# Order of the first two steps, place of the next x load, and time of the first group's norms in a four-layer kernel

## The chip, the cores and the metric

One core of one Trainium2 chip. The metric is device time in microseconds (us), median of 3 runs; lower is better. The program runs once from inputs in HBM to the output in HBM.

## What is computed

The input x is (T=4, B=8, N=512, D=512) in float32. Four layers, each `x = x + f(gn(x))`, where `gn` normalises over groups of two channels of axis 1 (4 groups) and the 512 x 512 plane:

```python
# layer 0, for each t and b: x is a 512 x 512 plane, 8 heads of 64
q, k, v = (lif(bn(gn(x) @ W.T)) for W in (Wq, Wk, Wv))     # spikes, 0 or 1
scores = q @ k.T / sqrt(512)                                # per head
scores = scores + bias_table[rel]                            # by distance of row and column
out = lif(bn((lif(scores @ v) * gate_scale + gate_shift) @ Wp.T))
x = x + out
x = x + conv13x13(gn(x))                                    # layer 1, one kernel per channel
x = x + quantised_conv3x3(gn(x))                            # layer 2, 8 to 8 channels
x = x + conv3x3(gn(x))                                      # layer 3, 8 to 8 channels
```

`lif` is a recurrence over t: `v = v + (x - v) / 2; spike = v >= 1; v = v * (1 - spike)`.

## The kernel before

Layer 0 takes the first 1840 us, and the change lies there. It runs over 32 steps, `steps = [(b, t) ...]` with t inner, so step n is plane b = n // 4, t = n % 4. A group is two planes b, that is 8 steps n.

Each step's products x W are made by `unit` (L566): two units "kv" (half of the rows of k and v each) and one unit "q". A unit uses a seven-product scheme on 2 x 2 blocks: it multiplies blocks of x, and sums of blocks, by blocks of W and sums of those. The seven products, in the order a1, a2, g7, b6, b5, e4, b3, go to PSUM tiles a, b, g, e, f, where ACT copies a running sum from one tile to another in between (L620 `a` from the constants, L625/L633 `b` from `a`, L643 `e` from `b`, L655 `f` from `b`), and DVE evicts the tiles into spikes (`evict`, L598 to L612). The sums of x are made by `sum_x` (L913 to L917, on DVE: first x5 and x7, then x6 and x3), those of W once by `sum_weights` (L387 to L390).

What a step needs beforehand: its x. `load` (L919) asks SP for it in four quarters (`xq`, L503, 4 times 256 KB, in pieces of 128 floats). The group statistics are counted from `xq` and from the other plane's rows (`xs`, L486) by DVE (L512), and `settle` (L869) ends in two small matmuls over the partitions (`gps_x`, L165) with DVE work between them. Then ACT normalises `xq` (L888, four instructions at slot 13 of the step before), DVE transposes it (L895, slots 14 and 17), and `sum_x` follows.

After every even n >= 2 comes `attend` for the two steps before: eight heads, each of 12 matmuls per table (`own_part`, L706) with a bias table `table_own` of 576 KB fetched from HBM (L436). Three tables are held. The first three heads' tables are there before the attention begins; that of head h + 3 is asked for when head h's matmuls are done. Below, "head 7" is the last of the eight. `project_out` (L773 to L834) is spread over slots of the two steps after it; ACT's copies L803 free the `xr` rows, whose buffers (pool `x0`, four tiles) the `xs` rows also use.

Once, at the start: `w_raw` is loaded and scaled (L358: v and k on DVE, q on GpSimd, POOL in the profile); `c_kv` and `c_step` (constants split in three bf16 parts, `shift_kv` L361, GpSimd; used by the matmul L650); `split_bias` (L392) makes the table of bias parts in HBM through DVE and DMAs on ACT's queue; `prepare_out` (L450) scales Wp during step 1, four row blocks of it in turn, each passed from ACT to GpSimd and back twice; `bands1` (L1084) builds layer 1's bands.

What sets the order: a scheduler places the instructions of each engine by data, buffers and the order in which the program calls them; `tc.issue_after(op)` keeps what is traced inside it behind `op` on `op`'s engine. All engines, and SP's and ACT's DMA queues, then work strictly in that order: an instruction that waits holds all those behind it. In a step, `for slot, op in enumerate(all_units(n))` gives the slots at which other work is traced.

Of the kernel before, what the change touches and what calls it, by code (L numbers as in the profile page):

```python
# [123 lines left out]
def network(ctx: ExitStack, tc: tile.TileContext, i: dict, out: bass.AP):  # L124
# [20 lines left out]
    def group_steps(  # L145
        stats, n_groups, n, mask, weights, psum, name, n_each=D // 2, bufs=2, then=None, share=None
    ):

        mean, m2 = stats[:, :, :, 1], stats[:, :, :, 2]
        gs = [P, n_groups]
        buf = small.tile([P, n_groups, n], F32, tag="gbuf", name=f"gbuf_{name}", bufs=1)
        part_sum = small.tile(gs, F32, tag="gsum", name=f"gsum_{name}")
        m = small.tile(gs, F32, tag=f"gmean_{bufs}", name=f"gmean_{name}", bufs=bufs)
        r = small.tile(gs, F32, tag=f"grstd_{bufs}", name=f"grstd_{name}", bufs=bufs)
        masks = mask.unsqueeze(1).to_broadcast([P, n_groups, n]) if mask is not None else None

        def over_partitions(src):
            nc.vector.tensor_reduce(part_sum, src, AX.X, ALU.add)  # L160
# [4 lines left out]
            nc.tensor.matmul(ps, lhsT=weights, rhs=part_sum, start=True, stop=True)  # L165
            yield
            return ps

        if mask is None:
            nc.vector.tensor_copy(m, (yield from over_partitions(mean)))  # L170
        else:
            nc.vector.tensor_mul(buf, mean, masks)
            nc.vector.tensor_copy(m, (yield from over_partitions(buf)))
        if then is not None:
            then(m)
        nc.vector.tensor_sub(buf, mean, m.unsqueeze(2).to_broadcast([P, n_groups, n]))
        nc.vector.tensor_mul(buf, buf, buf)
# [82 lines left out]
def layer0(  # L260
# [100 lines left out]
    def shift_kv(banks):  # L361
        rest = state.tile([3 * SQ, 2, HN], F32, tag="h_o", name="c_rest")
        for n in "kv":
            nc.vector.tensor_sub(
                rest[:, at_w[n], :], banks[n][: 3 * SQ, 1], c_kv[: 3 * SQ, at_w[n], :]
            )
        for z in range(3):
            for q in [slice(0, 3 * SQ)] if z == 0 else [slice(r * SQ, (r + 1) * SQ) for r in range(z, 3)]:
                nc.gpsimd.tensor_copy(c_step[q], rest[q])
                if z < 2:  # L370
                    nc.gpsimd.tensor_sub(rest[q], rest[q], c_step[q])


    def w_quarter(i, o):
# [7 lines left out]
    def sum_weights(first, end, engine):  # L382
# [7 lines left out]
        engine.tensor_sub(b12, b21, t2)  # L390

    def split_bias():  # L392

# [56 lines left out]
    def prepare_out():  # L450
# [2 lines left out]
        scratch = state.tile([P, 3, D], F32, tag="h_o", name="scale_wp")  # L453
        scale = scratch[:, 0, :]
        nc.scalar.copy(scale.rearrange("p (g v) -> p g v", g=PH), phases(along_free(a_rows, 3)))
        for k in range(NC):
            yield
            wp = scratch[:, 1 + k % 2, :]
            nc.scalar.mul(
                wp.rearrange("p (g v) -> p g v", g=PH), phases(wp_rows[k]), gate_scale[:, k : k + 1]  # L460
            )
            nc.gpsimd.tensor_mul(wp, wp, scale)
            yield
            nc.scalar.copy(wpT[0][:, k, :], wp)
            nc.gpsimd.tensor_sub(wp, wp, wpT[0][:, k, :].bitcast(F32))
            nc.scalar.copy(wpT[1][:, k, :], wp)
# [99 lines left out]
    def unit(kind, cc, n, got):  # L566
# [56 lines left out]
        if ahead:  # L623
            b = new("b")
            seeds.append(nc.scalar.copy(b, a).ins)  # L625
            mul(a, 2)
            evict(a, 0, 0)
            yield
        g = new("g")
        mul(g, 7, True)  # L630
        if not ahead:
            b = new("b")
            seeds.append(nc.scalar.copy(b, a).ins)  # L633
        twice.append(work.tile([P, 2, HN], F32, tag="twice", name="twice"))
# [4 lines left out]
        yield  # L639
        mul(b, 6)  # L640
        yield
        e = new("e")
        seeds.append(nc.scalar.copy(e, b).ins)  # L643
        if not ahead:
            mul(a, 2)
            evict(a, 0, 0)
            yield
        mul(b, 5)
        if kind == "kv":
            nc.tensor.matmul(  # L650
                b, lhsT=share, rhs=c_step, start=False, stop=True, skip_group_check=True
            )
        yield
        f = new("f")
        seeds.append(nc.scalar.copy(f, b).ins)  # L655
        mul(e, 4)
        evict(f, 1, 1)
        evict(e, 1, 0)
        yield
        mul(b, 3)  # L660
        evict(b, 0, 1)
        yield

    def shift_q(n):

# [187 lines left out]
    def first_norm(key):  # L853
# [3 lines left out]
        for first in (0, 2):  # L857
            with behind:
                next(steps)
            op = scale_weights("v", scales["v"], nc.vector, (first, first + 1))  # L860
            next(steps)
            behind = tc.issue_after(op)
        with behind:
            try:
# [89 lines left out]
    scales = {n: along_free(a_rows, "qkvp".index(n)) for n in "vkq"}  # L954
    scale_q = state.tile([P, D], F32, tag="h_p", name="scale_q")
    nc.scalar.copy(scale_q, scales["q"])
    with tc.issue_after(normed):
        load(0)
        second = load_x(1, 0, "xs")
# [4 lines left out]
    constants = {}  # L964
    for n in "kv":
        constants[n] = along_free(c_rows, "qkvp".index(n)).rearrange("p (o e) -> p o e", o=2)
        nc.scalar.copy(c_kv[:, at_w[n], :], constants[n][:, 0])
    normalise(0)
    transpose(0, 0)
    transpose(0, 1)  # L970
    scale_weights("k", scales["k"], nc.vector)
    sum_x(0, 0)
    summed = sum_x(0, 1)
    sum_weights(0, 2, nc.vector)
    scale_weights("q", scale_q, nc.gpsimd)
    sum_weights(2, 3, nc.gpsimd)

    def all_units(n):
        if n == 0:
# [16 lines left out]
    for n in range(last + 3):  # L996
# [10 lines left out]
        if n <= last:  # L1007
# [1 line left out]
                spikes = new_spikes()  # L1009
            spikes["k"] = spiking.tile([P, NC, D], F8, tag="k", name="k")  # L1010
            g, j = divmod(n, PAIR * T)
            if n > 0:
                with tc.issue_after(fetched[-1]) if n % 2 == 0 else ExitStack():
                    load(n + 1)
            if j == 2 and g > 0:
                norm1(g - 1, ps_1)
            if g == 0 and 0 < n < T - 1:
                statistics(0, n + 1, 0, as_rows(xs[n + 1]))
                statistics(0, n + 1, 1, load_x(1, n + 1, "xs"))
            while due:  # L1020
                settle(due.pop())
            if n > 0:
                next_group(n - 1)
        if n == 1:
            preparing = prepare_out()
            banding = bands1(tc, i, band1d, w_sum, eye, ps_1, state)
        for slot, op in enumerate(all_units(n)):
# [9 lines left out]
                    statistics(0, 1, 1, load_x(1, 1, "xs"))  # L1037
            if n == 0 and slot == 0:
                with tc.issue_after(summed):
                    shift_kv(constants)  # L1040
            if n == 0 and slot == 7:
                with tc.issue_after(potentials[1]), tc.issue_after(seeds[0]):
                    parts = split_bias()
                    next_group(-1)
                with tc.issue_after(loads[-1]):
                    for h in range(H):
                        nc.sync.dma_start(tables_x[h], table_rows(h, 0, 1))
# [2 lines left out]
                    shift_q(n - 1)  # L1050
            if n == 1:
                with tc.issue_after(seeds[-1]):
                    if slot % 2 == 0:
                        next(preparing, None)
                    if slot in (11, 19):
                        next(banding, None)
            if slot == 13 and n <= last:
                add_halves(spikes, steps[n][1])
                with tc.issue_after(seeds[-1]):
# [24 lines left out]
def bands1(tc, i, band1d, w_sum, eye, psum, state):  # L1084
# [8 lines left out]
    def part(n_part, n):  # L1093
# [5 lines left out]
    w1 = part(K1, B * n_w).rearrange("k (c d) -> k c d", c=B)  # L1099
    c13 = part(K1, PH * n_p).rearrange("k (f j) -> k f j", f=PH)  # L1100
    rows = part(K1, B)
    nc.scalar.dma_start(
        c13, i["c13"].rearrange("k (f j) -> k f j", f=PH)[:, :, (W1_OUT - 1) * PH :][:, :, :n_p]
    )
    nc.vector.memset(w1, 0.0)
    taps = w1[:, :, PH - 1 : PH - 1 + K1]
    nc.scalar.dma_start(taps, i["w1"].rearrange("k (c d) -> k c d", c=B))
    nc.scalar.dma_start(
        eye.rearrange("p s m -> p (s m)"), i["c128"][:K1_P, i["c128"].shape[1] - SHIFTS * M1 :]
    )  # L1110
    nc.vector.memset(zeros, 0.0)
    rest = band1d.rearrange("p (r m) -> p r m", r=W1_OUT)
    nc.scalar.dma_start(rest, zeros.unsqueeze(1).to_broadcast([K1_P, W1_OUT, P]))
    yield

    ps = psum.tile([n_p, P], F32, tag="misc", name="ps_band")
    for f in range(PH):
# [7 lines left out]
    nc.scalar.dma_start(  # L1125
        bass.AP(band1d.tensor, band1d.offset, [[row, n_p], [PH * row + P, W1_OUT], [1, P]]),
        band.unsqueeze(1).to_broadcast([n_p, W1_OUT, P]),
    )
# [625 lines left out]
```

## Time and profile before

| what | us |
|---|---|
| median of 3 runs | 2715.78 |
| lowest, highest | 2710.00, 2716.22 |
| the profiled execution's own time | 2710.35 |
| its span on the core | 2708.6 |
| layer 0: first matmul of a unit | 29.70 |
| first attention begins on PE (L706) | 134.98 |
| last attention's end, about | 1835 |

PE is TensorE, DVE VectorE, ACT ScalarE, POOL GpSimd, SP SyncE. In a timeline line stand the start, the duration of the merged run, engine, source line, operation, out<-in, shape and count; in brackets, the engine's idle time just before it and what ended it. An fp32 matmul instruction of 512 columns has two records here, so one product of a unit is "x4", 1.88 us. ACTq and SPq are the queues in which ACT and SP issue DMAs. Where DMA is named as releaser, the data landed last.

### The profile page before, as it was taken

The page shows a single profiled execution, that of the slowest core. Times are in us where ns is not written, and L with a number is a line of the kernel's source. Part 1 is how long each engine was busy: PE and PEld are TensorE (multiplying, and loading weights), DVE is VectorE, ACT ScalarE, POOL GpSimd, SP SyncE. Part 2 cuts the span into 40 slices and gives each one's busy share as a digit, 9 for nine tenths or more (in the row PEclk, how much of TensorE's full clock was granted, in tenths as well). Part 3 has the DMA queues.
Part 4 walks back from the last instruction along what each step waited for, and adds up shares of the span by engine and source line. Part 5 has one row for each costly group of instructions (what it writes and reads, how often), then busy time and mean ns, then how long its engine had stood idle before and what let it go on. Part 6 is the DMA issues. An engine that isn't in the chain of part 4 may idle for free. (4 is left out here: it accounts for less than half of the span.)

```text
span 2708.6 us, 49604 instructions
## 1 busy us (share of the span) xinstructions
PE 2599.6 (96%) x18124; PEld 1506.2 (56%) x18124; DVE 1918.7 (71%) x4054; ACT 1238.3 (46%) x2093; POOL 756.0 (28%) x2040
## 2 busy tenths in 40 slices
PE   7899999999999999999999999998999999689999
PEld 3566566665666656666567666664333333344447
DVE  7877878778688787877877768756555556665550
ACT  1454454555445545445554554543111211466663
POOL 4322224123132222312312322223111111454540
PEclk9999999999999999999999999998999999899999
DMA  5553443544435444354442442446877778567755
GB/s 135 154 145 97 131 128 105 139 113 113 126 98 147 109 121 134 79 149 107 125 126 71 118 108 81 122 118 152 219 188 213 207 217 219 141 191 210 212 164 154
DMA packets 420664, 385.02 MB, mean 142 GB/s; under 512 B 22675, under 2 KB 339843, under 8 KB 420307
## 3 DMA queue, kind: packets, MB, share of 16 engines
q1 hardware_dynamic: 361696, 306.46, 43.8%
q0 software_dynamic: 16448, 51.27, 5.2%
q10 hardware_dynamic: 42275, 24.12, 3.2%
q8 instruction: 142, 2.33, 0.4%
q14 instruction: 103, 0.84, 0.1%
HBM read 278.09 MB, written 103.67 MB: 141 GB/s over the span
## 5 line engine op out<-in xcount | busy, mean ns | idle before, releaser
L1192 PE MATMUL ps_conv<-x,bt 112*64 112x512 f32 x2048 | 451.5, 595 | 6.4 <-DMA x<-x 6.4
L823 POOL COPY x1s<-x1s 128x1 f32<-128x1 f32 x1000 | 187.9, 241 | 649.8 <-DVE x1s L811 636.8
L1192 PEld LDWEIGHTS ps_conv<-x,bt 112*64 112x64 f32 x2048 | 149.2, 135 | 297.9 <-issue 293.8
L787 PE MATMUL ps_out<-wp,so 128*128 128x512 f32 x1024 | 303.9, 440 | 5.9 <-ACT ps_out L784 4.0
L554 PE MATMUL ps_kv_a<-w_raw,x_raw 128*128 128x512 f32 x512 | 252.8, 612 | 13.9 <-DVE w_raw L358 9.2
L1199 ACT ACTIVATE xo<-ps_conv,off 128x512 f32<-128x512 f32 x128 | 87.7, 687 | 378.3 <-PE ps_conv L1192 315.6
L787 PEld LDWEIGHTS ps_out<-wp,so 128*128 128x128 f32 x1024 | 193.9, 191 | 108.8 <-ACT ps_out L784 38.8
L554 PE MATMUL ps_kv_b<-w_sums,x_sum 128*128 128x512 f32 x512 | 246.6, 602 | 4.8 <-DVE x_sum L916 2.8
L1632 PE MATMUL ps_conv<-x,band_t 32*32 32x512 f32 x6144 | 230.2, 597 | 1.0 <-ACT o L1672 1.0
L638 POOL TENSOR_TENSOR h_kv<-h_kv,twice 128x512 f32<-128x512 f32 x96 | 123.6, 1307 | 380.4 <-ACT twice L635 379.8
L706 PE MATMUL ps_own<-table_own,v 128*128 128x256 bf16 x1536 | 193.3, 275 | 24.1 <-DMA table_own<-bias_parts 21.1
L706 PEld LDWEIGHTS <-v 128*128 128x128 fp8e4 x1536 | 148.2, 98 | 66.7 <-DMA table_own<-bias_parts 32.5
L1214 POOL DMA_DIRECT2D x<-xo x128 | 71.4, 564 | 345.6 <-ACT xo L1199 337.3
L742 ACT COPY ps_f<-ps_own 64x512 f32<-64x512 f32 x256 | 142.9, 558 | 49.7 <-PE ps_own L706 21.6
L1527 DVE SCALAR_TENSOR_TENSOR x<-ps_conv,inv,x 128x512 f32<-128x512 f32 x128 | 95.2, 750 | 98.8 <-PE ps_conv L1491 90.1
L554 PEld LDWEIGHTS ps_kv_a<-w_raw,x_raw 128*128 128x128 f32 x512 | 96.8, 195 | 111.1 <-issue 95.3
L1632 PEld LDWEIGHTS ps_conv<-x,band_t 32*32 32x32 f32 x6144 | 118.1, 103 | 70.2 <-issue 47.1
L554 PEld LDWEIGHTS ps_kv_b<-w_sums,x_sum 128*128 128x128 f32 x512 | 95.9, 191 | 103.2 <-issue 85.0
L803 ACT COPY x1s<-xr 128x256 f32<-128x256 f32 x250 | 151.8, 659 | 1.6 <-DMA x<-x1s 1.6
L1154 DVE SCALAR_TENSOR_TENSOR bt<-band,r,eye 112x64 f32<-112x64 f32 x128 | 31.6, 370 | 165.5 <-PE ps_conv L1192 164.0
L1491 PE MATMUL ps_conv<-xq,band 64*64 64x512 bf16 x1536 | 125.7, 400 | 21.5 <-DVE x L1527 15.4
L783 ACT CAST so<-q 128x512 fp32r<-128x512 fp8e4 x128 | 78.9, 618 | 142.9 <-PE ps_out L787 138.9
(257 smaller groups left out, 5060.4 us busy)
## 6 DMA issues: line engine op xcount, KB each, us to landing
table_own<-bias_parts SPq DMA_DIRECT2D x128, 576.0 KB
x<-x SPq DMA_DIRECT2D x64, 917.0 KB
xq<-in_x SPq DMA_DIRECT2D x128, 256.0 KB
xr<-in_x SPq DMA_DIRECT2D x128, 256.0 KB
x<-x1s POOLq DMA_DIRECT2D x125, 262.0 KB, 2.8
out<-o SPq DMA_DIRECT2D x120, 256.0 KB
xs<-in_x SPq DMA_DIRECT2D x112, 256.0 KB
x<-x SPq DMA_DIRECT2D x128, 224.0 KB
```

The source lines that it names most:

```text
L554: mm = nc.tensor.matmul(ps, lhsT=x[:, kk, cc * P : (cc + 1) * P], rhs=w[:, :2, kk, :], start=start and kk == 0, stop=kk == 1, skip_group_c ...
L638: nc.gpsimd.tensor_add(h, c if t == 0 else h, twice[0])
L706: nc.tensor.matmul(out, lhsT=src[:, c, h].rearrange("p t e -> p (t e)"), rhs=table[:, z, u : u + HN], start=start and c == 0 and z == 0, s ...
L742: nc.scalar.copy(final[j][a][two * DH : (two + 1) * DH, :], rows[a * DH : (a + 1) * DH, :])
L787: nc.tensor.matmul(ps, lhsT=tokens[:, k, :], rhs=wpT[z][:, k, :], start=False, stop=k == NC - 1 and z == 1, skip_group_check=True,)
L803: op = nc.scalar.copy(halves[z][1], by_phase[:, two, :])
L823: nc.gpsimd.tensor_copy(x1[:, f, u : u + n], x1[:, fm, um - n + 1 : um + 1][:, ::-1])
L1192: mm = nc.tensor.matmul(ps[q * M1 : (q + 1) * M1, :], lhsT=bt[:, z, :], rhs=xt[:, w0 : w0 + N_PS1, z : z + NV], start=z == 0, stop=z == SH ...
L1199: nc.scalar.activation(xo[:, a, :], ps, AF.Identity, bias=off[:, t : t + 1])
L1491: mm = nc.tensor.matmul(ps[half, :], lhsT=w["band2"][halves[b], kind, dx, :], rhs=xq[halves[b], j % 2, dx : dx + PH, :], start=dx == 0 and ...
L1527: nc.vector.scalar_tensor_tensor(inner, ps, w["inv"], x, op0=ALU.mult, op1=ALU.add, accum_out=sums[:, 0, :] if summed else None,).ins
L1632: mm = nc.tensor.matmul(ps[c * QP : (c + 1) * QP, :], lhsT=band[g * QP : (g + 1) * QP, int(last), dx, :], rhs=src[:, dx : dx + PH, :], sta ...
```

## The change

1. Opening: `scale_weights("k")` is put ahead of the sums of x on DVE, and these behind it alternate with `sum_weights(0, 2)`; the constants' matmuls (`along_free`) and copies for q and c are spread into the first norm; `shift_kv` stands behind those; the scaling and sums of q's weights are called behind `shift_kv`'s last GpSimd instruction.
2. `split_bias` and the `table_x` loads go from slot 7 to slot 14 of step 0; `next_group(-1)` stays at slot 7.
3. `prepare_out` takes two row blocks at a time, so that the GpSimd work of one lies beside ACT's work of the other; it ends before slot 14.
4. The DMAs of `bands1` go from ACT's queue to SP's.
5. At even n, `load(n + 1)` is called after `next_group(n - 1)` and stands on SP behind its first `xs` load, where there is one; before, it stood behind the last table fetched so far. At odd n it is still called first.
6. For n = 1 and 2 the norm of step n + 1 is no longer settled where its rows are asked for; for the first group's two planes (n < 8) all open norms are settled at slot 9. `yield` now hands out the matmul to which this is tied.
7. In `unit`, the copy L633 is called ahead of the g product.

In the built program this moves on SP, at the eleven attentions that have an `xs` load behind them (n = 2 to 22): before, five tables, the four `xq`, one `xs`, three tables among the other `xs`; after, eight tables, `xs`, `xq`, `xs`, `xq`, `xs`, `xs`, `xq`, `xq`. At the four attentions from n = 24 on nothing moves.

```diff
@@ group_steps
-            nc.tensor.matmul(ps, lhsT=weights, rhs=part_sum, start=True, stop=True)
-            yield
+            mm = nc.tensor.matmul(ps, lhsT=weights, rhs=part_sum, start=True, stop=True)
+            yield mm.ins
@@ prepare_out
-        for k in range(NC):
+        def scaled(k):
+            nc.scalar.mul(
+                wps[k].rearrange("p (g v) -> p g v", g=PH), phases(wp_rows[k]),
+                gate_scale[:, k : k + 1],
+            )
+            nc.gpsimd.tensor_mul(wps[k], wps[k], scale)
+
+        def first_part(k):
+            nc.scalar.copy(wpT[0][:, k, :], wps[k])
+            nc.gpsimd.tensor_sub(wps[k], wps[k], wpT[0][:, k, :].bitcast(F32))
+
+        def second_part(k):
+            nc.scalar.copy(wpT[1][:, k, :], wps[k])
+
+        for k in (0, 2):
             yield
...
+            scaled(k)
             yield
...
+            first_part(k)
+            scaled(k + 1)
+            yield
+            second_part(k)
+            first_part(k + 1)
+            yield
+            second_part(k + 1)
@@ first_norm
-            next(steps)
+            with tc.issue_after(next(steps)):
+                if first == 0:
+                    scales["q"] = along_free(a_rows, 2)
+                    nc.scalar.copy(scale_q, scales["q"])
+                else:
+                    for n in "kv":
+                        ps = along_free(c_rows, "qkvp".index(n))
+                        constants[n] = ps.rearrange("p (o e) -> p o e", o=2)
+                        nc.scalar.copy(c_kv[:, at_w[n], :], constants[n][:, 0])
@@ layer0, opening
-    scale_weights("k", scales["k"], nc.vector)
-    sum_x(0, 0)
-    summed = sum_x(0, 1)
-    sum_weights(0, 2, nc.vector)
-    scale_weights("q", scale_q, nc.gpsimd)
-    sum_weights(2, 3, nc.gpsimd)
+    op = scale_weights("k", scales["k"], nc.vector)
+    with tc.issue_after(op):
+        sum_x(0, 0)
+        sum_x(0, 1)
+    summed = sum_weights(0, 2, nc.vector)
@@ layer0, at the start of step n
-            if n > 0:
-                with tc.issue_after(fetched[-1]) if n % 2 == 0 else ExitStack():
-                    load(n + 1)
+            if n % 2 == 1:
+                load(n + 1)
...
-            if g == 0 and 0 < n < T - 1:
-                statistics(0, n + 1, 0, as_rows(xs[n + 1]))
-                statistics(0, n + 1, 1, load_x(1, n + 1, "xs"))
             while due:
                 settle(due.pop())
             if n > 0:
+                at = len(loads)
                 next_group(n - 1)
+                if n % 2 == 0:
+                    with tc.issue_after(loads[at] if at < len(loads) else fetched[-1]):
+                        load(n + 1)
+                if g == 0 and n < T - 1:
+                    statistics(0, n + 1, 0, as_rows(xs[n + 1]))
+                    statistics(0, n + 1, 1, load_x(1, n + 1, "xs"), later=True)
@@ layer0, slots
-                    shift_kv(constants)
+                    last_step = shift_kv(constants)
+                with tc.issue_after(last_step):
+                    scale_weights("q", scale_q, nc.gpsimd)
+                    sum_weights(2, 3, nc.gpsimd)
             if n == 0 and slot == 7:
                 with tc.issue_after(potentials[1]), tc.issue_after(seeds[0]):
+                    next_group(-1)
+            if n == 0 and slot == 14:
+                with tc.issue_after(potentials[-1]), tc.issue_after(seeds[-1]):
                     parts = split_bias()
-                    next_group(-1)
...
-                    if slot % 2 == 0:
+                    if slot < 14:
                         next(preparing, None)
-                    if slot in (11, 19):
+                    if slot in (12, 19):
                         next(banding, None)
+            if n <= last and slot == 9 and steps[n][0] < PAIR:
+                with tc.issue_after(op):
+                    while due:
+                        settle(due.pop(0))
@@ bands1, all five DMAs
-    nc.scalar.dma_start(
+    nc.sync.dma_start(
```

More of the change, by code (lines that the diff above doesn't have):

```diff
@@ L368, in shift_kv @@
             for q in [slice(0, 3 * SQ)] if z == 0 else [slice(r * SQ, (r + 1) * SQ) for r in range(z, 3)]:
-                nc.gpsimd.tensor_copy(c_step[q], rest[q])
+                op = nc.gpsimd.tensor_copy(c_step[q], rest[q])
                 if z < 2:
                     nc.gpsimd.tensor_sub(rest[q], rest[q], c_step[q])
+        return op.ins
     def w_quarter(i, o):
@@ L389, in sum_weights @@
         engine.tensor_sub(t2, b22, t1)
-        engine.tensor_sub(b12, b21, t2)
+        return engine.tensor_sub(b12, b21, t2).ins
     def split_bias():
@@ L455, in prepare_out @@
         nc.scalar.copy(scale.rearrange("p (g v) -> p g v", g=PH), phases(along_free(a_rows, 3)))
-        for k in range(NC):
-            yield
[L458 to L462, printed above, removed]
-            yield
-            nc.scalar.copy(wpT[0][:, k, :], wp)
-            nc.gpsimd.tensor_sub(wp, wp, wpT[0][:, k, :].bitcast(F32))
-            nc.scalar.copy(wpT[1][:, k, :], wp)
+        wps = [scratch[:, 1 + k % 2, :] for k in range(NC)]
+        def scaled(k):
[10 more added lines that the diff above has]
+        for k in (0, 2):
+            yield
+            scaled(k)
+            yield
+            first_part(k)
[5 more added lines that the diff above has]
+            second_part(k + 1)
         yield
@@ L625, in unit @@
             seeds.append(nc.scalar.copy(b, a).ins)
-            mul(a, 2)
+            op = mul(a, 2)
             evict(a, 0, 0)
-            yield
+            yield op
         g = new("g")
-        mul(g, 7, True)
         if not ahead:
@@ L633, in unit @@
             seeds.append(nc.scalar.copy(b, a).ins)
+        op = mul(g, 7, True)
         twice.append(work.tile([P, 2, HN], F32, tag="twice", name="twice"))
@@ L638, in unit @@
             nc.gpsimd.tensor_add(h, c if t == 0 else h, twice[0])
-        yield
-        mul(b, 6)
-        yield
+        yield op
+        yield mul(b, 6)
         e = new("e")
@@ L644, in unit @@
         if not ahead:
-            mul(a, 2)
+            op = mul(a, 2)
             evict(a, 0, 0)
-            yield
-        mul(b, 5)
+            yield op
+        op = mul(b, 5)
         if kind == "kv":
-            nc.tensor.matmul(
+            op = nc.tensor.matmul(
                 b, lhsT=share, rhs=c_step, start=False, stop=True, skip_group_check=True
-            )
-        yield
+            ).ins
+        yield op
         f = new("f")
         seeds.append(nc.scalar.copy(f, b).ins)
-        mul(e, 4)
+        op = mul(e, 4)
         evict(f, 1, 1)
         evict(e, 1, 0)
-        yield
-        mul(b, 3)
+        yield op
+        op = mul(b, 3)
         evict(b, 0, 1)
-        yield
+        yield op
     def shift_q(n):
@@ L953, in layer0 @@
     c_rows = as_rows_of(c_half.rearrange("p n c -> p (n c)"), rows[:, 1])
-    scales = {n: along_free(a_rows, "qkvp".index(n)) for n in "vkq"}
+    scales = {n: along_free(a_rows, "qkvp".index(n)) for n in "vk"}
+    constants = {}
     scale_q = state.tile([P, D], F32, tag="h_p", name="scale_q")
-    nc.scalar.copy(scale_q, scales["q"])
     with tc.issue_after(normed):
@@ L963, in layer0 @@
         statistics(0, 0, 1, second)
[L964 to L967, printed above, removed]
     normalise(0)
@@ L1106, in bands1 @@
     taps = w1[:, :, PH - 1 : PH - 1 + K1]
-    nc.scalar.dma_start(taps, i["w1"].rearrange("k (c d) -> k c d", c=B))
-    nc.scalar.dma_start(
+    nc.sync.dma_start(taps, i["w1"].rearrange("k (c d) -> k c d", c=B))
+    nc.sync.dma_start(
         eye.rearrange("p s m -> p (s m)"), i["c128"][:K1_P, i["c128"].shape[1] - SHIFTS * M1 :]
@@ L1112, in bands1 @@
     rest = band1d.rearrange("p (r m) -> p r m", r=W1_OUT)
-    nc.scalar.dma_start(rest, zeros.unsqueeze(1).to_broadcast([K1_P, W1_OUT, P]))
+    nc.sync.dma_start(rest, zeros.unsqueeze(1).to_broadcast([K1_P, W1_OUT, P]))
     yield
@@ L1124, in bands1 @@
     row = W1_OUT * P
-    nc.scalar.dma_start(
+    nc.sync.dma_start(
         bass.AP(band1d.tensor, band1d.offset, [[row, n_p], [PH * row + P, W1_OUT], [1, P]]),
```

## The prediction

> **What bounds the kernel.** I read the page first. PE is busy for 96% of the span, so only PE's idle time and slow matmuls can be won.
>
> ```profile
> PE 2599.6 (96%) x18124; PEld 1506.2 (56%) x18124; DVE 1918.7 (71%) x4054; ACT 1238.3 (46%) x2093; POOL 756.0 (28%) x2040
> ...
> PE   7899999999999999999999999998999999689999
> ...
> PEclk9999999999999999999999999998999999899999
> ```
>
> The thin slices are the first three and those behind layer 0. The change reaches only layer 0, so I cut that by stage: to the first attention, its first pair of steps, the attentions whose SP order moves, the rest.
>
> ```profile
> 0.00:135.00 135.00, 107.00 (x340) 60.98 (x341) 104.80 (x208) 37.18 (x60) 49.24 (x43) 0.97 0.59 145
> 135.00:262.00 127.00, 119.22 (x531) 77.80 (x530) 96.72 (x202) 61.26 (x107) 34.04 (x86) 0.96 0.42 113
> 262.00:1330.00 1068.00, 1050.33 (x4629) 689.76 (x4627) 855.61 (x1791) 553.67 (x964) 278.82 (x790) 1.00 0.45 122
> 1330.00:1830.00 500.00, 489.73 (x2180) 323.15 (x2179) 368.10 (x767) 262.46 (x458) 135.18 (x372) 1.00 0.40 107
> ```
>
> The second number is the length, the third PE's busy time: 28.0 us idle before the first attention, 7.8 behind it, 17.7 in the long stretch. PE's waits in 262 to 1330 name the last:
>
> ```profile
> PE ps_own L706 <- DMA table_own<-bias_parts: 12.5, 12, 2.9
> ```
>
> So the prize is two piles: about 28 us at the start, and bias tables that come late. PE's timeline of the start shows the first pile, with what held it (idle time in the bracket):
>
> ```profile
> 29.70 3.75 PE L554 MATMUL ps_kv_a<-w_raw,x_raw 128*128 128x512 f32 x4 [9.16 <-DVE w_raw L358]
> 41.88 1.99 PE L554 MATMUL ps_kv_a<-w_raw,x_raw 128*128 128x512 f32 x4 [1.05 <-ACT ps_kv_b L625]
> 79.67 3.56 PE L554 MATMUL ps_kv_a<-w_raw,x_raw 128*128 128x512 f32 x4 [2.40 <-ACT ps_kv_a L620]
> 106.14 0.38 PE L165 MATMUL gps_x<-gsum_x,avg 128*128 128x1 f32 x2 [2.15 <-DVE gsum_x L160]
> 124.47 2.00 PE L560 MATMUL ps_q_b<-x_sum,w_sums 128*128 128x256 f32 x8 [2.35 <-ACT ps_q_e L643]
> ```
>
> **Tables.** In the attention that begins at 702.0, head 7's table is asked for at 714.27, the four xq 0.5 us behind it:
>
> ```profile
> 714.27 0.36 SPq L436 DMA_DIRECT2D table_own<-bias_parts  x1
> ```
>
> and PE's timeline shows where it is waited for:
>
> ```profile
> 721.89 2.74 PE L706 MATMUL ps_own<-table_own,v 128*128 128x256 bf16 x12 [2.86 <-DMA table_own<-bias_parts]
> ```
>
> Here a rule speaks against the change. The Trainium skill (DMA: Bandwidth & Descriptors, section Queues, rings and completion order) says that on each DMA engine descriptors are consumed in ring order; then xq, issued later on SP's ring, could not delay the table, and moving it would give nothing. The row: DMA stands nearly still at 713.5 (15 to 23 GB/s, so all earlier tables have landed), and from 714.4 until PE goes on at 721.9 some 1.87 MB move, of which heads 6 and 7 are 2 x 576 KB. So about 0.7 MB of xq went ahead of the table's last bytes; at the 200 to 220 GB/s of that stretch this is 3.3 us, more than the wait of 2.86. I follow the row.
>
> With xq behind the tables, head 7's 576 KB flow alone: latency 1.5 us, then at the 340 to 370 GB/s seen at 714.6 some 1.7 us, landing near 718 where PE asks at 719.0. The new companion, the next pair's first table, is asked for only when head 5's matmuls are done (717.1), so its bytes begin near 718.6. Head 7's waits in the eleven attentions that change: 2.25, 1.76, 0.58, 0.21, 1.17, 2.86, 0.38, 0.67, 0, 2.26, 0 = 12.1 us. Waits of heads 5 and 6 (1.37, 0.58, 0.46 ...) stay, as do those from 1330 on (0.81, 0.36, 1.61, 0.78, 2.12): nothing is reordered there.
>
> What a wait costs beyond itself: after 2.25 and 2.86 us of idling, 12 matmuls took 2.74 instead of 1.48 us, twice 1.26. The Trainium skill (TensorE: Matmul & The Clock Gate, Part 1) would have the clock fall only after an idle window of about 3.4 us; by it the pile is 12.1, by the row 14.6. The row decides, though after 2.26 us at 1166.99 it was 1.52. With a tenth kept back: **-13 us**, from 0 to -15.
>
> What xq then costs. Its first quarter goes out behind xs 1, which waits for ACT's first L803; its last behind xs 4. Before, in the attention from 370 on, the last xs went out at 404.31 (the two there take 0.94), so the last xq goes at about 406 instead of 384 and lands by 409. Its reader is ACT:
>
> ```profile
> 418.16 2.94 ACT L888 ACTIVATE xq<-xq,shift,grstd_x 128x512 f32<-128x512 f32 x4
> ```
>
> Nine us of cover, so nothing is paid; without it, each us late is a us of PE in each of eleven steps. Behind xq on SP wait the xr loads and the small rows L831; xr stood at 408.29 anyway.
>
> **The opening.** Scaling k comes ahead of the four sums (25.49 to 28.15) and c_rest (0.74): the first product starts at 26.3 instead of 29.70, **-3.4**. Its slow clock (3.75 for x4 against 1.88) stays. The split of the bias leaves the kv units: ACT no longer stands behind the bias_table DMA (6.69 us, to 41.26), **-1.1**; the two xq quarters of step 1 which waited 15.3 us for the same DMA come early, and DVE has some 5 us less there, so the gps_x waits of 0.90 and 0.72 go, **-1.6**.
>
> Two new lateness risks. First, c_rest on DVE now stands behind the sums of W: GpSimd's c_step chain begins at 37.4 instead of 28.96. Before it took 11.0 us, of which 5.84 were two casts beside DVE's sums, where one such cast later took 0.75; without that, 6.4. It ends between 43.8 and 48.4; PE asks for it (L650) at 44.4. I take 0.5 us, between 0 and 4 plus 1.5 of slow clock. Behind it on GpSimd are q's scaling (5.26) and sums (5.93), to 56, where the q products want the sums from 59 on: covered by 3 us.
>
> Second, the bias split is now in step 0's q unit, in front of the x sums of step 1. Its eight DVE pieces (L397 to L413) are about 3 us. DVE took 10.3 us from the first transpose (74.07) to x6 (84.4), now 13.3; the transposes start near 67.6, so x6 is there at about 81. PE ends step 0 at 70.7 instead of 77.2 and reaches b6 at 76.7: a wait of 4.3 plus 1.5 of slow clock, in place of the 2.40 plus 1.7 at 79.67 (ps_kv_a was held by the Wp DMAs on ACT, which now come after it). The net there is **+1.7**.
>
> Step 1, from 79.67 to 134.98, has some 44 us of PE work. Gone: the ACT wait at 124.47 (2.35), held by a GpSimd answer of 4.05 us, and most of 2.15 + 1.5 at 106.14, since the norm's DVE steps are no longer among evictions. Come in: Wp's blocks in pairs put two scalings of 1.25 us between the h_q shifts (2.55) and the next ps_kv_a copy; that copy is ready 5.6 us behind ps_kv_f's, with 2.7 us of product e and b3 in between: +2.9, as against 0.61; two norms settle together, about +1. The sum is **-2.5**. The band DMAs leave ACT (6.05 us of standing at 110.25, but PE did not wait there): 0. On SP they stand ahead of the first three tables, 40 us before use. The `prepare_out` copies that wait for GpSimd in front of ps_kv_e are covered by the x6 wait; without that they would cost about 3.
>
> Start: -3.4 - 1.1 - 1.6 + 0.5 + 1.7 - 2.5 = **-6.4**, say -7 with the small gaps that go with it. If both risks cost full, -1; if none costs, -13.
>
> **Steps 2 and 3.** The norm of step 3 settles in the q unit (from 193) instead of at 182.27 (1.48), and ACT then normalises between g and e: perhaps 2 us new, against 1.48 and part of the x_sum wait at 214.69 (2.81, with 1.6 of slow clock behind it). DVE is full there both times. I take -1, from +4 to -4. Slot 9 in steps 4 to 7, and L633's earlier call: 0, within 1 either way (gps_x costs 0.3 to 0.7 where seen).
>
> **The sum.** -13 - 7 - 1 = -21 us on the profiled execution's 2710.35, that is 2689. The median lies 5.4 above that execution (one of three runs was at 2710, two at 2716), so on the median it would be 2695. I state 2691.
>
> **Rivals.** *Opening alone* (head 7 stays late because the next pair's tables take xq's place in the DMA engines): for it, three tables are 1.7 MB against xq's 1 MB; against it, their late issue. -8: 2704. *Tables alone* (DVE and POOL give back the opening: c_step 4 + 1.5, x6 6 + 1.5): DVE is busy 87% of 40 to 100, which speaks for it. -13: 2699. *Neither*: the waits are only renamed: 2712. *Slower*: x too late. Quarters of xq behind four xs, each behind a buffer that ACT's L803 frees, miss the 9 us of cover; then PE waits at the next step's first products by the excess, eleven times. At 2 us excess it eats the 21 won; at 4 us, +44 - 21 gives 2735. Against it: the xs rows went out by 405 in before's own trace.
>
> **Numbers.** Forecast 0.56, tables alone 0.20, opening alone 0.13, neither 0.07, slower 0.04. The forecast's own bounds: tables -15 and start -13 with steps 2 and 3 at -3 give 2679; the weak ends of the two rivals reach 2706. Outside lie neither, slower and small tails. A change under 0.3% (8 us: above 2707.6) can't be told from none: faster 0.87, same 0.09, slower 0.04.
>
> **What would show it.** First unit matmul near 26.3, first attention near 127 instead of 134.98. From 262 to 1330 table waits of 2 to 4 us instead of 12.5, no 2.74 us runs. L888 not waiting for xq. A wait for x_sum L916 near 77 to 82, one for ps_kv_a in step 1. I am wrong if PE waits for x_raw at the begin of odd steps, if head 7's wait stays above 1 us, or if L650 waits for c_step by 3 us or more.

## The result, and the profile after

The changed kernel takes 2708.12 us (median of 12 runs, 2706.01 to 2712.37), the kernel before 2712.35 in the same rounds: a ratio of 0.9982, 95% interval 0.9974 to 0.9991. That is 4.2 us less by the medians and 4.9 by the ratio (2.4 to 7), where 21 were forecast; 2708 lies above the 2706 that the prediction's bounds reached. The profiled execution of after took 2708.08, with a span of 2706.3.

The same four stretches as before, in the kernel after (length, then PE's busy time):

```profile
0.00:135.00 135.00, 110.35 (x346) 63.09 (x347) 106.59 (x217) 37.32 (x60) 47.68 (x44) 0.95 0.58 142
135.00:262.00 127.00, 119.49 (x550) 77.42 (x548) 98.05 (x201) 62.77 (x110) 34.17 (x86) 0.99 0.43 120
262.00:1330.00 1068.00, 1050.75 (x4616) 689.68 (x4615) 874.33 (x1787) 554.45 (x965) 289.06 (x791) 1.00 0.44 121
1330.00:1830.00 500.00, 490.50 (x2193) 323.89 (x2192) 367.41 (x766) 262.67 (x459) 132.40 (x370) 1.00 0.41 108
```

PE's idle time is 24.7, 7.5, 17.3 and 9.5 us, against 28.0, 7.8, 17.7 and 10.3. In the long stretch it is the same although the tables come earlier; PE's waits there say what took their place:

```profile
PE ps_own L722 <- DMA table_own<-bias_parts: 5.1, 6, 1.3
PE gps_x L165 <- DVE gsum_x L160: 3.3, 2, 2.0
PE gps_x L165 <- DVE gsum_x L162: 2.5, 2, 1.3
...
PE ps_kv_a L571 <- ACT ps_kv_a L637: 2.1, 5, 0.5
```

Before, the two gps_x rows were smaller, and ps_kv_a was not waited for:

```profile
PE gps_x L165 <- DVE gsum_x L160: 1.4, 2, 0.7
PE gps_x L165 <- DVE gsum_x L162: 0.8, 2, 0.4
```

Tables fell from 12.5 to 5.1 us. In the attention that lost 2.86 us before, SP now asks for eight tables in a row and for xq far behind them, and head 7 waits 1.31 us with no slow matmuls after it. The SP queue of after there, and PE:

```profile
707.71 16.48 SPq L437 DMA_DIRECT2D table_own<-bias_parts  x8
731.87 0.35 SPq L503 DMA_DIRECT2D xs<-in_x  x1
732.28 0.42 SPq L520 DMA_DIRECT2D xq<-in_x  x1
```

```profile
722.32 1.48 PE L722 MATMUL ps_own<-table_own,v 128*128 128x256 bf16 x12 [1.31 <-DMA table_own<-bias_parts]
```

PE's timeline of the start, after:

```profile
26.28 3.75 PE L571 MATMUL ps_kv_a<-w_raw,x_raw 128*128 128x512 f32 x4 [2.00 <-ACT ps_kv_a L637]
...
61.80 0.38 PE L165 MATMUL gps_x<-gsum_x,avg 128*128 128x1 f32 x2 [2.57 <-DVE gsum_x L160]
62.04 3.66 PE L577 MATMUL ps_q_g<-x_raw,w_sums 128*128 128x256 f32 x8
...
87.00 3.75 PE L571 MATMUL ps_kv_b<-w_sums,x_sum 128*128 128x512 f32 x4 [5.01 <-DVE x_sum L940]
91.42 3.78 PE L571 MATMUL ps_kv_b<-w_sums,x_sum 128*128 128x512 f32 x4 [0.66 <-ACT ps_kv_e L659]
...
101.46 1.98 PE L571 MATMUL ps_kv_a<-w_raw,x_raw 128*128 128x512 f32 x4 [2.01 <-ACT ps_kv_a L637]
```

The first product comes at 26.28 instead of 29.70, as forecast; the first attention begins at 134.78 instead of 134.98. The lead was waited away in between. The first product takes 3.75 us in both kernels, which the prediction put down to a slow clock; the row of the granted clock reads 1.00 there (26.3 to 30.0), so what slows it stays open. Behind the waits of 2.57 and 5.01 us the row does show it: 0.52 from 62.0 to 65.5 and 0.50 from 87.0 to 90.7.

### The profile page after: what moved, and what is told of

It reads as the page before. It is cut to its first block, busy times and chain, and to the rows that moved or that the text cites. A ratio compares the mean times of both kernels' runs of the same rounds, so it can differ in the third digit from the quotient of the medians.

```text
span 2706.3 us, 49605 instructions
## 1 busy us (share of the span) xinstructions
PE 2601.4 (96%) x18124; PEld 1502.4 (56%) x18124; DVE 1938.4 (72%) x4054; ACT 1239.0 (46%) x2093; POOL 762.1 (28%) x2040
## 5 line engine op out<-in xcount | busy, mean ns | idle before, releaser
L839 POOL COPY x1s<-x1s 128x1 f32<-128x1 f32 x1000 | 194.2, 248 | 736.0 <-DVE x1s L827 703.8
L655 POOL TENSOR_TENSOR h_kv<-h_kv,twice 128x512 f32<-128x512 f32 x96 | 126.4, 1339 | 340.3 <-ACT twice L652 339.8
```

Source lines behind the costliest of these rows:

```text
L839: nc.gpsimd.tensor_copy(x1[:, f, u : u + n], x1[:, fm, um - n + 1 : um + 1][:, ::-1])
```

## Experiments

Ratios are to the kernel before, with 95% intervals; 0.001 is 2.7 us. "Second attention" is when PE begins it in the one profile of each kernel: 257.8 before, 255.6 after. Five kernels have the same order up to the first attention (before, before_again, xq_only, xq11, xq_all), and their profiles begin it at 131.8 to 136.7: one profile does not settle less than 5 us there.

**The tables: part 5 alone.** xq_only, on the kernel before, leaves out the first of the eleven attentions:

```diff
-            if n > 0:
+            if n % 2 == 1 or n == 2:
                 with tc.issue_after(fetched[-1]) if n % 2 == 0 else ExitStack():
                     load(n + 1)
...
             if n > 0:
+                at = len(loads)
                 next_group(n - 1)
+                if n % 2 == 0 and n > 2:
+                    with tc.issue_after(loads[at] if at < len(loads) else fetched[-1]):
+                        load(n + 1)
```

> Before, with only the four xq of the step after next put behind all eight tables, in the ten attentions that begin at 257.8 to 1260.3 (the first attention is left as it was). Theory (the table gain is real and is given back elsewhere by the change): table waits from 262 to 1330 fall from 12.5 to 3 to 5 us, head 7 no longer waits, no wait for x_raw; 8 to 10 us less than before, near 2703. Rival (head 7 stays late, or late x takes the gain): table waits stay above 9 us, or a new wait of 1 us or more per odd step at the step's first products; within 3 us of before.

2699.13 us, 0.9946 (0.9931 to 0.9961): 14.6 us less than before, more than the whole change. Its table waits from 262 to 1330:

```profile
PE ps_own L706 <- DMA table_own<-bias_parts: 6.8, 6, 1.4
```

Head 7's wait does not vanish (up to 1.4 stay), so the waits fall less than I expected, yet the time falls by more. The ten intervals from the second to the twelfth attention take 1104.0 us against 1112.3, 8.3 less; the rest of the 14.6 lies in the spread of the start, or in runs that the one profile is not like. xq11 is part 5 whole: the first attention too, with the statistics of step 3 called behind its load (against xq_only):

```diff
-            if n % 2 == 1 or n == 2:
-                with tc.issue_after(fetched[-1]) if n % 2 == 0 else ExitStack():
-                    load(n + 1)
+            if n % 2 == 1:
+                load(n + 1)
...
-            if g == 0 and 0 < n < T - 1:
+            if n == 1:
...
-                if n % 2 == 0 and n > 2:
+                if n % 2 == 0:
...
+                if n == 2:
+                    statistics(0, n + 1, 0, as_rows(xs[n + 1]))
+                    statistics(0, n + 1, 1, load_x(1, n + 1, "xs"))
```

> The kernel before with part 5 of the change alone, whole: xq behind the tables in the first eleven attentions, the last four as before; the statistics of step 3 follow the load. Theory (the table waits are the one gain of the change, and parts 1 to 4 neither win nor lose): 2696 to 2699, table waits of the first attention under 0.7, and as fast as or within 2 us of the changed kernel without its parts 6 (from step 4 on) and 7, 2694.7. Rival (the opening is worth 3 us or more): slower than that kernel by 3 us or more.

2696.92 us, 0.9948 (0.9931 to 0.9965). As expected, and 2.2 us above the kernel l633 below by the medians, 1.1 by the ratios. That is no sign of an opening worth 3 us or more, though the intervals leave room for one.

xq_all is xq11 and, besides, moves xq in the last four attentions ahead of nearly all tables:

```diff
-                    with tc.issue_after(loads[at] if at < len(loads) else fetched[-1]):
+                    with tc.issue_after(loads[at] if at < len(loads) else loads[-NC]):
```

> Before, with the xq of all fifteen attentions moved: in the first eleven behind the eight tables, as in after; in the last four, which have no xs, ahead of nearly all tables of the attention. Theory: on top of the kernel with ten moved (2699), head 7's wait in the first attention goes (2.25 and 1.26 of slow matmuls), and in the last four head 7's waits of 0.5 to 2.1 go, while head 3 may wait for its table by 1 to 2 us there: 2 to 5 us less than 2699. Rival (xq ahead of the tables delays them as much as xq among them): table waits from 1330 to 1830 stay at 5 to 7 us, within 2 us of 2699.

2700.15 us, 0.9965 (0.9955 to 0.9975): no gain over xq_only's 2699. PE's waits from 1330 to 1830 in it show the exchange:

```profile
PE ps_f L750 <- ACT ps_f L742: 5.6, 10, 1.1
PE ps_own L706 <- DMA table_own<-bias_parts: 3.2, 6, 1.6
```

Table waits are 3.2 instead of 6.4, but PE now waits 5.6 us for ACT's copies in the same attentions. The rival's size was right, though not its mechanism.

**Part 6 in steps 4 to 7: slot 9.** no_slot9 keeps the settling in mid step for steps 1 to 3:

```diff
-            if n <= last and slot == 9 and steps[n][0] < PAIR:
+            if n < T and slot == 9:
```

> After, with the settling at slot 9 kept for steps 1 to 3 only (in steps 4 to 7 the norm is settled at the start of the next step, as before). Theory (in slot 9 the two small matmuls wait for DVE work of two SBUF inputs that stands behind GpSimd's pair of additions, 2.3 to 2.9 us, and TensorE runs slow after it): the gps_x waits of 1.97 and 1.35 in steps 5 and 7 and the slow matmuls behind them go, 6 us less than after, near 2702. Rival (the norm costs the same wherever it is settled): the waits come back at the start of the next steps, within 2 us of after.

2702.92 us, 0.9960 (0.9945 to 0.9975), 0.0022 or 6 us below after (the intervals meet only at their ends). The two intervals concerned shrink from 112.5 and 113.0 to 108.5 and 111.3. What had happened in after, in step 5: PE, then DVE, then GpSimd:

```profile
345.10 0.38 PE L165 MATMUL gps_x<-gsum_x,avg 128*128 128x1 f32 x2 [1.97 <-DVE gsum_x L160]
345.34 3.65 PE L803 MATMUL ps_out<-wp,so 128*128 128x512 f32 x8
```

```profile
341.53 0.17 DVE L176 TENSOR_TENSOR gbuf_x<-st,gmean_x 128x16 f32<-128x16 f32 x1
341.74 2.89 DVE L177 TENSOR_TENSOR gbuf_x<-gbuf_x 128x16 f32<-128x16 f32 x1
```

```profile
342.09 2.50 POOL L655 TENSOR_TENSOR h_kv<-h_kv,twice 128x512 f32<-128x512 f32 x2
```

A product over 16 elements per partition (L177) takes 2.89 us instead of 0.17. It ends when GpSimd's two additions end (344.59), and the second small matmul waits for it with all of PE's queue behind it. The Trainium skill (SBUF — State Buffer, section Who interferes with whom) says that a DVE instruction with two SBUF inputs and a GpSimd instruction that reads SBUF exclude each other. These rows agree, but for the start: L177 is recorded 0.35 us ahead of the additions. In step 7 it is L176 that is long, 2.27 us from 456.73, and it ends with GpSimd's additions, which run from 456.45 to 458.95. slot12 does the same settling where GpSimd is idle:

```diff
-            if n <= last and slot == 9 and steps[n][0] < PAIR:
+            if n < 8 and slot == (9 if n < T else 12):
```

> After, with the settling of steps 4 to 7 at slot 12 instead of slot 9 (steps 1 to 3 unchanged), so that it is still in mid step but no longer right behind the g product, where GpSimd's two additions L655 run. Theory (the wait is DVE's two-input work standing behind GpSimd's pair): the gps_x waits of 1.97 and 1.35 and the slow matmuls behind them go, and no 2 us run of L176 or L177 is left; 4 to 6 us less than after, as the kernel without it at 2703. Rival (DVE is simply full in mid step, or the two small matmuls wait there for any reason): waits of 1 us or more stay, within 2 us of after.

2701.69 us, 0.9966 (0.9955 to 0.9976). DVE and PE of slot12 in step 5:

```profile
351.00 0.17 DVE L176 TENSOR_TENSOR gbuf_x<-st,gmean_x 128x16 f32<-128x16 f32 x1
...
351.68 0.17 DVE L177 TENSOR_TENSOR gbuf_x<-gbuf_x 128x16 f32<-128x16 f32 x1
```

```profile
353.05 0.38 PE L165 MATMUL gps_x<-gsum_x,avg 128*128 128x1 f32 x2
```

No wait, the same work in mid step: the place beside GpSimd was the cost, not mid step.

**The start: the bias split.** bias7 puts `split_bias` back to slot 7 of step 0; bias_late calls it behind `sum_x(1, 1)`, the last x sum of step 1. Both take the `table_x` loads along. The edit of bias_late:

```diff
-            if n == 0 and slot == 14:
-                with tc.issue_after(potentials[-1]), tc.issue_after(seeds[-1]):
-                    parts = split_bias()
...
-        sum_x(n + 1, 1)
+        summed = sum_x(n + 1, 1)
+        if n == 0:
+            with tc.issue_after(summed), tc.issue_after(seeds[-1]):
+                parts = split_bias()
```

> After, with the bias split back at slot 7 of step 0. Theory A (DVE sets the start: all that stands on it before the x sum x6 must be done, in whatever order): x6 is made at 86 as in after, the first attention begins at 134 to 136, within 2 us of after. Theory B (the place of the split in front of x6 is what costs, as the prediction had it): x6 at 83, the wait of 5.0 falls to 2, first attention at 130 to 132, 3 to 5 us less than after.

> After, with the bias split behind the x sums of step 1, so that its eight DVE pieces (some 3.4 us) are not in front of x6. Theory A (DVE sets the start): x6 at about 83 instead of 86.9, the wait for it falls from 5.0 to 1 to 2 us and the slow matmuls behind it go; first attention at 130 to 132 unless GpSimd and ACT work on Wp, which now starts later, gives a part back; 2 to 4 us less than after. Rival (x6 is late by the arrival of x or by the norm, not by DVE's work): x6 stays within 1 us of 86.9, no gain.

bias7: 2709.38 us, 0.9990 (0.9981 to 1.0000). Its x6 begins on DVE at 86.43 (after: 85.70), its first attention at 136.5, as theory A had it: the wait only moves. PE now waits 3.05 and 3.86 us for gps_x in step 0, and no more for x6. bias_late: 2706.65, 0.9982 (0.9975 to 0.9990), the same as after. PE of bias_late:

```profile
83.15 1.96 PE L571 MATMUL ps_kv_b<-w_sums,x_sum 128*128 128x512 f32 x4 [0.95 <-DVE x_sum L940]
...
98.85 3.68 PE L571 MATMUL ps_kv_b<-w_sums,x_sum 128*128 128x512 f32 x4 [2.78 <-ACT ps_kv_b L649]
114.93 0.59 PE L165 MATMUL gps_x<-gsum_x,avg 128*128 128x1 f32 x2 [5.75 <-DVE gsum_x L160]
```

x6 does come 4 us earlier, its wait is 0.95 instead of 5.01, but ACT's copies and the norm take it back in step 1 (2.78 and 5.75), and the first attention begins at 137.9, not at 130 to 132 as I expected.

**The start: less DVE work.** light counts the statistics of the first group's norms for t = 1 to 3 (DVE counts them in steps 0 to 2) over 64 of 512 columns, so these norms are other numbers:

```diff
-            nc.vector.bn_stats(stats[:, pair, c, :], xt[c])
+            nc.vector.bn_stats(stats[:, pair, c, :], xt[c][:, :n])
...
-        count(xt, norms[key], pair)
+        count(xt, norms[key], pair, 64 if g == 0 and t > 0 else N)
```

> After, with the statistics of steps 1 to 7 of the first group's planes counted over 64 of 512 columns, so that the norms there are other numbers: some 4 us of DVE work less in each of steps 0 to 2. Theory (DVE sets the start): in step 0 the gps_x wait of 2.57 and the x6 wait of 5.01 shrink to under 1 and under 2, x6 is made at 82 to 83, and the first attention begins 4 to 8 us earlier than 134.8. Rival (arrival of x, ACT's copies or GpSimd's answers set it): first attention within 2 us of 134.8.

2699.63 us, 0.9966 (0.9953 to 0.9979). First attention 131.4 (3.4 earlier, less than the 4 to 8 expected, and within the spread of profiles), second 245.1. PE waits for x6 at 83.90, 2.71 us, so that wait shrank less than I expected. The gps_x wait shrank only from 2.57 to 1.93. DVE's work sets much of the first four steps, as a second attention 10.5 us earlier shows, where three profiles of one order spread over 2.5; behind x6 ACT's copies hold PE too (ps_kv_a, 3.20 at 97.95).

**The opening alone.** opening_only is after with parts 5, 6 and 7 put back:

```diff
-            if n % 2 == 1:
-                load(n + 1)
+            if n > 0:
+                with tc.issue_after(fetched[-1]) if n % 2 == 0 else ExitStack():
+                    load(n + 1)
...
-            if n <= last and slot == 9 and steps[n][0] < PAIR:
-                with tc.issue_after(op):
-                    while due:
-                        settle(due.pop(0))
```

(`next_group`, the statistics and L633 also stand as in before.)

> Parts 1 to 4 of the change alone (opening, place of the bias split, Wp in pairs, bands on SP); xq, norms and L633 as before. Theory (DVE sets the start, so the opening's earlier first product is waited away again): first unit matmul at 26.3, first attention at 132 to 137, second attention at 255 to 259, within 3 us of before. Rival (the opening does win its 6 to 7 us, and the norms of steps 2 and 3 or slot 9 lose them): 5 to 7 us less than before.

2705.58 us, 0.9979 (0.9963 to 0.9995), 5.7 us less than before with an interval of 1.4 to 10. First attention 133.4, second 250.4: neither account fits throughout. The first attention is the theory's, the time the rival's, and the second attention is earlier than both had it. before_again is the kernel before, once more:

> The kernel before, unchanged, for a second profile of it: first attention between 133 and 137 and second between 254 and 258 if the first profile (135.0, 257.8) is typical; 251 or less would mean that one profile cannot tell 5 us at the start.

2711.20 us; 135.6 and 255.6. With xq_only, whose order is that of before up to there (136.7, 255.3), profiles of one order spread over 2.5 us at the second attention.

**Part 7: the copy L633.** l633 takes it out of no_slot9; xq_l633 puts it into xq_only:

```diff
         g = new("g")
-        op = mul(g, 7, True)
         if not ahead:
             b = new("b")
             seeds.append(nc.scalar.copy(b, a).ins)
+        op = mul(g, 7, True)
```

(This is xq_l633, with `mul` as it stands there; l633 is the reverse.)

> The kernel with slot 9 kept for steps 1 to 3 only, and besides with the copy L633 (b from a) back behind the g product. Theory: the small new waits at the begin of a pair's first step (gps_x 1.25 in three groups, ps_kv_a 0.39 to 0.51 five times) come from another order of ACT's copies; with the old order the gps_x ones fall to 0.3 to 0.7 and the others to 0, 2 to 3 us less than the 2703 of that kernel. Rival (they come from the place of xq or from the settling): they stay, within 1.5 us.

> The kernel before with ten xq moved, and besides with part 7 of the change alone (copy L633 ahead of the g product). Theory (L633's place costs by itself, in every step): gps_x waits of 1.25 at three groups' begins and ps_kv_a waits of 0.4 to 0.5 come in, 3 to 4 us more than with ten xq alone (2699), near 2702.5. Rival (it costs only together with the changed norms): within 1.5 us of 2699.

l633: 2694.71 us, 0.9944 (0.9927 to 0.9962), 8 us below no_slot9's median and 4.3 below by the ratios, with intervals that overlap. xq_l633: 2692.86, 0.9936 (0.9917 to 0.9955), not slower than xq_only but 2.7 faster by the ratios: my theory falls there. The waits I named do come with part 7 on either opening (gps_x 1.25 in three groups, ps_kv_a 0.4 several times; in l633 gps_x waits 0.44 and 0.71, and ps_kv_a none), some 3 to 4 us in all from 262 to 1830. The table waits in that stretch also differ: 9.6 us in xq_l633 against 14.5 in xq_only, but 9.1 in no_slot9 against 12.2 in l633. xq_l633 further begins its second attention at 250.2, 5 us before xq_only. Why, no run here shows; the sign of part 7 with the old opening stays open.

**Parts 6 and 7 taken out.** no6 is after without part 6; no6_no7 also without part 7 (L633 as above); xq_norms is xq11 with part 6 for steps 1 to 3 only. no6 takes out

```diff
-                if g == 0 and n < T - 1:
-                    statistics(0, n + 1, 0, as_rows(xs[n + 1]))
-                    statistics(0, n + 1, 1, load_x(1, n + 1, "xs"), later=True)
...
-            if n <= last and slot == 9 and steps[n][0] < PAIR:
-                with tc.issue_after(op):
-                    while due:
-                        settle(due.pop(0))
```

(with the statistics called and settled for n = 1 and 2 as in xq11) and xq_norms puts in

```diff
+            if 0 < n < T and slot == 9:
+                with tc.issue_after(op):
+                    while due:
+                        settle(due.pop(0))
```

(with the statistics for n = 1 and 2 left open until then).

> After without part 6 (norms settled as before in all steps; opening, xq and L633 of the change kept). Theory C (the norms in mid step of steps 1 to 3 give back what the opening wins): second attention at 249 to 252 instead of 255.6, time near 2691. Theory D (L633 gives it back): second attention stays at 254 to 257, time near 2697 to 2702.

> After without parts 6 and 7 (opening and xq alone). Theory C: second attention at 249 to 252, near 2691, as no6. Theory D: 249 to 252 here but not in no6. Neither (the opening wins nothing and the 250.4 was the spread of a profile): 254 to 257, near 2696.

> The kernel before with part 5 whole (xq behind the tables in eleven attentions) and the part 6 of steps 1 to 3 only; old opening, no settling at slot 9 from step 4 on. Theory C: second attention 2 to 5 us later than the 252.9 of the same kernel without the norms, near 2700. Rival: within 2 us of 252.9 and of 2697.

no6: 2699.60, 0.9960 (0.9947 to 0.9972), second attention 252.3. no6_no7: 2694.88, 0.9941 (0.9921 to 0.9961), 254.4. xq_norms: 2699.79, 0.9966 (0.9955 to 0.9976), 260.6. On the new opening, part 6 of steps 1 to 3 costs nothing in time (no6 and no_slot9 both 0.9960, no6_no7 and l633 0.9941 and 0.9944); on the old one 0.0018, 5 us, with intervals that overlap. Theory C is not shown, and D neither.

The ladder by ratio, each rung a kernel measured:

| kernel | parts | ratio | us against before |
|---|---|---|---|
| xq11 | 5 | 0.9948 | -14 |
| no6_no7 | 1 to 5 | 0.9941 | -16 |
| no6 | 1 to 5, 7 | 0.9960 | -11 |
| after | all | 0.9982 | -5 |

Each ratio is uncertain by 2 to 5 us to either side, so the rungs of 2 and 5 us (the opening, part 7) are not clear of it; the last, part 6, agrees with the trace of slot 9. xq_l633, l633 and no6_no7 (2692.9 to 2694.9) beat both before and after, and can't be told from each other, nor from part 5 alone (xq11).

## Why the prediction was wrong, by its steps

- **Tables, -13: right in mechanism and about right in size.** Part 5 gives 14 us by ratio, 8.3 by the trace from the second to the twelfth attention, where the forecast had 9.9 of waits and some slow matmuls. Head 7's waits were to vanish; up to 1.4 us stay. The row that I followed against the argument from ring order was the right guide: xq behind the tables moved them forward. But head 7's table does not flow alone, as I had it. In the attention shown, head 6's is asked for 1.3 us before it (714.93 and 716.24), and the core moves 1.18 MB, the size of both, from 716.0 to 720.5; PE goes on at 722.3, 6.1 us after the request instead of 3.2. What fills the last 1.8 us the trace doesn't say. So my sign of being wrong, a wait of head 7 above 1 us, came true there (1.31), with 5.1 us of table waits where 2 to 4 were expected.
- **x late, the slower rival: right that it does not come.** In after the last xq goes out at 405.7 (forecast: about 406), and ACT's L912 has no idle time before it.
- **"Slot 9 in steps 4 to 7, and L633's earlier call: 0, within 1 either way": the step that failed, first by slot 9, 6 us.** I costed the norm by the 0.3 to 0.7 us of gps_x "where seen", and did not ask what runs on GpSimd in that slot. The norm's first small matmul stands one product behind the g product, whose result starts L655. The waits of 1.97 and 1.35 are what it costs, with slow matmuls behind the first (3.65 us at a granted clock of 0.55, where eight such records took 2.12 behind the second), and slot12 removes them.
- **The same step, by L633's call:** some 3 to 4 us of small waits in the traces, 4 to 5 by ratio on the new opening, in two pairs whose intervals overlap; not settled on the old one.
- **First product at 26.3, -3.4, and the ACT wait, -1.1: right.** 26.28, and no wait for ps_kv_b at 37.
- **gps_x in step 0, -1.6: wrong, +2.7.** One wait of 2.57 replaces 0.90 and 0.72, and the q product behind it takes 3.66 instead of 1.89. The statistics on DVE begin only at 56.24, behind the evictions of the kv units.
- **c_step, +0.5: 0 in after.** Its GpSimd chain runs from 37.06 to 44.34, and L666 starts at 44.40 without a wait. It was close: in bias7 and bias_late L666 waits 1.75 and 1.52 us for it.
- **x6, +1.7: wrong, +5.4.** A wait of 5.01 and 4.5 of slow matmuls (3.75 and 3.78 instead of 1.88, and 0.7 in the two runs behind) stand against 2.40 and 1.7 before. I let DVE follow PE's lead and put its transposes at 67.6; they begin at 72.23. (PE's lead itself was summed 0.4 too large: 77.2 less my terms of 6.1 is 71.1, not 70.7.) DVE is busy for 24.95 of the 26.80 us from 45.4 to 72.2, so an earlier PE brings it forward by little; in light, with less work on DVE, PE has x6 3 us earlier. x6 is ready at 86.86, later than the 84.46 of before. Part of DVE's time there is GpSimd's doing: its q scaling and sums now lie beside more of the kv evictions, as DVE's lines of after show:

```profile
46.99 1.35 DVE L621 TENSOR_SCALAR v<-v_kv 128x256 fp8e4<-128x256 f32 x1
48.26 1.75 DVE L629 SCALAR_TENSOR_TENSOR h_kv<-v_kv 128x512 f32<-128x512 f32 x1
...
55.43 0.28 DVE L621 TENSOR_SCALAR v<-v_kv 128x256 fp8e4<-128x256 f32 x1
55.63 0.68 DVE L629 SCALAR_TENSOR_TENSOR h_kv<-v_kv 128x512 f32<-128x512 f32 x1
```

  and GpSimd's of after:

```profile
44.43 5.04 POOL L358 TENSOR_TENSOR w_raw<-w_raw,scale_q 128x512 f32<-128x512 f32 x4
```

  Beside GpSimd the same two instructions take 3.1 us, without it 1.0. From 46.1 to 55.5 this adds 5.7 us to the evictions. The kernel before lost 3.9 us by the same count (its L604 takes 1.35 and L612 1.75 at 45.4 and 46.7, and two instructions of the bias split are slowed too), so the move itself adds some 2 us. No run moves GpSimd's chain alone, so this share is read from the traces, not tested. I had moved the chain by 8 us and looked only at who waits for its result, not at who shares its time.
- **Step 1, -2.5: right, -3.9.** Waits of 2.35 and 2.15 (with slow matmuls) are gone, ps_kv_a waits 2.01 instead of 0.61.
- **Sum of the start:** -3.4 - 1.1 + 2.7 + 5.4 - 3.9 = -0.3, measured -0.2. The forecast's "-7" is missed by the terms gps_x and x6. The rival "tables alone" had it: DVE gives the opening back, by x6, though not by c_step. In time the opening is worth 2 us on top of part 5 and 5.7 alone, both uncertain by 4 or more.
- **Steps 2 and 3, -1: can't be told.** The stretch from the first to the second attention was 122.9, 120.0 and 118.7 us in before, before_again and xq_only, which have one order there; after has 120.8.

So the table gain was there, part 6 and (on this opening, by overlapping intervals) part 7 took most of it, and the start's own gain was lost by the two mis-sized terms. The measured 2708 lies nearest the rival "neither" (2712), but by luck: that rival had the table waits renamed, and part 5 alone gains 14 us. No rival had a case in which a part put at 0 costs 6 us.

## What to carry to other kernels

Before moving small work, look at what the other engines do in its new place: here a DVE product of 0.17 us took 2.89 beside GpSimd's additions, and since PE's queue stood behind it, PE paid. Where one engine is nearly always busy (DVE for 93% of 45 to 72 us here), an earlier start on another can be waited away again, as a lead of 3.4 us shrank to 0.2. Measure the parts of a bundle one by one: one of seven parts held nearly all of the gain here, one gave 6 us back, and a second seems to have given 4 to 5.

## Of the hardware, not expected

What a wait of 2 to 3 us costs TensorE in slow matmuls behind it varied here from nothing to 5 us. PE at the begin of step 1, first in xq_norms, then in xq_all, and the same 16 us of each as a window (the eighth column is the granted clock):

```profile
80.51 3.11 PE L554 MATMUL ps_kv_a<-w_raw,x_raw 128*128 128x512 f32 x4 [2.66 <-ACT ps_kv_a L620]
83.55 2.07 PE L346 MATMUL ps_free<-rows,ident 16*128 16x128 f32 x8
85.55 3.78 PE L554 MATMUL ps_kv_g<-w_sums,x_raw 128*128 128x512 f32 x4
```

```profile
79.00:95.00 16.00, 13.83 (x25) 6.18 (x26) 10.89 (x23) 4.53 (x7) 3.76 (x3) 0.68 1.09 255
```

```profile
80.09 1.98 PE L554 MATMUL ps_kv_a<-w_raw,x_raw 128*128 128x512 f32 x4 [2.73 <-ACT ps_kv_a L620]
82.00 1.15 PE L346 MATMUL ps_free<-rows,ident 16*128 16x128 f32 x8
```

```profile
79.00:95.00 16.00, 14.25 (x38) 6.51 (x39) 13.60 (x26) 8.16 (x14) 6.01 (x4) 1.00 1.10 258
```

A wait of 2.66 us was followed by products of 3.11 and 3.78 us, one of 2.73 by products of 1.98, nearly full speed (1.88): 0.68 of the clock against 1.00. That may be a good part of why the first attention begins at 131.8 to 136.7 in profiles of one order, and a single profile cannot settle 3 us there.
